# A two-layer graph network with attention: each load of q and k writes one of the two copies

## The chip, the cores and the metric

The kernel runs on one core of a Trainium2 chip. The metric is device time of one execution in microseconds (us). The core has a matrix engine (PE), a vector engine (DVE), an activation engine (ACT), a general engine (POOL, GpSimd) and a synchronisation engine (SP), which here only issues DMA transfers; the transfers themselves are carried out by 16 DMA engines that all queues share.

## The reference, cut to what matters

There are 3,327 nodes with 128 features and a dense adjacency matrix of zeros and ones. Layer 0 normalises the features, multiplies them by the transposed adjacency and by two small weights, normalises over the nodes and adds the result to x. Layer 1, in which nearly all the time goes, is an attention:

```python
q = (x @ Wq.T).reshape(d, n, h)          # d = 128 groups, n = 3327, h = 8
k = (x @ Wk.T).reshape(d, n, h)
v = (x @ Wv.T).reshape(d, n, h)
a = jnp.einsum('dnh,dmh->dnm', q, k) * scale
a = a + spatial_encoding + edge_encoding  # both are adj
a = jax.nn.softmax(a, axis=2)
out = jnp.einsum('dnm,dmh->dnh', a, v)
out = out.reshape(n, h * d)
return out @ Wo.T                         # added to x by the caller
```

So there are 128 independent attentions of 3,327 queries over 3,327 keys with a depth of only 8, and every score gets twice the adjacency entry added.

## The kernel before, in words

**Operands.** q and k are each split into a rounded part and a remainder (`projection`, lines 230 to 241), which are stored in DRAM as the 16 rows of `qT` and `kT`: rows 0 to 7 are the rounded part, rows 8 to 15 the remainder, one row for each h. A row holds all 128 groups, one after the other, and two rows are 425,984 numbers apart. In SBUF a group takes 32 partitions. Its q tile holds rounded, rounded, remainder, remainder; its k tile holds rounded, remainder, rounded, remainder. One product over 32 partitions thus sums all four part products. Every row of qT and kT is therefore needed twice in SBUF, and this repeat is what the change touches.

**Loops.** `attention` goes through 32 iterations i (`NG`), each for four groups (`G`), which lie in the four strips of 32 partitions. An iteration has seven blocks y of 480 queries (the last has 448) and in each 13 steps s, so 91 steps. A step treats two of the 26 chunks of 128 keys, for all four groups, as four (chunk, pair of groups) products in PSUM (`product`, line 785). Two or three of the four get the adjacency added by DVE from a tile `at` (line 925), and ACT takes the exponential of all of them at once (d, line 970). The others go through ACT first (f, line 934), and POOL multiplies them by weights `wt`, exponentials of the adjacency stored in DRAM as `wd` (line 937). PE then weighs v with the results, three steps later (`weigh`, line 670).

**Order.** The order of the instructions on each engine is written out by hand. SP issues its DMAs in program order, and a DMA that has to wait for a buffer or for data holds all behind it. `fetch` issues the loads of `at` (line 773, four buffers) and `wt` (line 769, three buffers) two steps ahead. `loads` (lines 167 to 202) makes the list of what the next iteration needs: for each half of the keys four loads of k into a staging tile `ks` (a pool with one buffer), then POOL copies (`sort`, line 194) that bring it into the order of the chunks in the k tile; v after the first half; and the q loads dealt out between the copies. All its DMAs have line 172. The list is spread evenly over the steps of the iteration, from step 4 on (step 39 in iteration 0):

```python
while pending and (total - len(pending)) * (SU * len(qblocks) - FROM[i] - 4) <= k * total:
    pending.pop(0)()
```

The q and k tiles have two sets, used in turn. In the same iteration the projections for the groups after the next are made piece by piece (`go_on`), and their stores to kT, qT and v1 (lines 247 and 222) stand in SP's order too. They wait for POOL, which splits the values.

**Start.** For iteration 0 `first_loads` (lines 873 to 901) loads the whole k of the four groups, straight into an unused tile, then the first 512 columns of q (line 883), then v; ACT, DVE and POOL sort k together (line 894). The rest of q (`others`, line 915) follows two loads a step from the third step on. In iteration 0 the weights wd of later blocks are also made: a load t (line 814), an exponential by ACT (line 819) and a store (line 806).

The helper `q_loads` gives two loads for a group (line 138 on): each writes 16 partitions from 8 rows with a leading repeat of 2. `k_loads` gives one load that writes 32 partitions from 16 rows with a leading repeat of 2.

Of the kernel before, what the change touches and what calls it, by code (L numbers as in the profile page):

```python
# [9 lines left out]
F32 = mybir.dt.float32  # L10
# [8 lines left out]
N = 3327  # L19
D = 128  # L20
H = 8
# [25 lines left out]
def tile_two_layer_gnn(  # L47
# [34 lines left out]
    kT = dram.tile([2 * H, TP], F32, name="kT")  # L82
# [55 lines left out]
    def q_loads(q, p0, d, n0=0, n=NP):  # L138

        qs = qT[:, bass.ds(d * N + n0, n)].rearrange("(a h) n -> a h n", h=H)  # L140
        return [
            (
                q[p0 + a * 2 * H : p0 + (a + 1) * 2 * H, n0 : n0 + n].bitcast(F32),
                qs[a].unsqueeze(0).to_broadcast([2, H, n]),
            )
            for a in range(2)
        ]

    def k_loads(k, p0, d, n0, n):
        ks = kT[:, bass.ds(d * N + n0, n)]  # L150
        return [(
            k[p0 : p0 + 4 * H].bitcast(F32), ks.unsqueeze(0).to_broadcast([2, 2 * H, n])
        )]

    def v_loads(v, d):
        W = NC * (H + 1)
# [10 lines left out]
    def loads(tiles, d):  # L167
# [6 lines left out]
        def batch(b):  # L174
            return d + b if b else d

        qs = [dma(*a) for b in range(G) for a in q_loads(q, 32 * b, batch(b))]
        vv = [dma(*a) for a in v_loads(v, d)]
        todo = []
        for half in range(2):  # L180

            ks = ksp.tile([P, NP // 2], F32R, name="ks")
            for b in range(G):
                todo += [
                    dma(*a)
                    for a in k_loads(ks, 32 * b, batch(b), half * (NP // 2), NP // 2)
                ]
            todo += vv if half == 0 else []
            todo += [qs.pop(0) for _ in range(2) if qs]
            for c in range(0, NC, 4):  # L190
                n = min(4, NC - c)

                def sort(ks=ks, c=c, n=n, half=half):
                    nc.gpsimd.tensor_copy(  # L194
                        k[:, c : c + n, half * 64 : half * 64 + 64],
                        ks.bitcast(F32).rearrange("g (p c) -> g c p", c=NC)[:, c : c + n, :],
                    )

                todo.append(sort)
                if qs:  # L200
                    todo.append(qs.pop(0))
# [107 lines left out]
    with tc.tile_pool(name="l0", bufs=1) as l0, tc.tile_pool(  # L309
# [16 lines left out]
        cols = l0.tile([P, 4], F32, name="cols")  # L326
# [162 lines left out]
        for c in range(NC):  # L489
            a = tiles[c]  # L490
# [37 lines left out]
            i = c - 2 * NQ - 5  # L528
# [4 lines left out]
        for n0 in range(0, NB, NB // 2):  # L533
            a = ap.tile([P, 7 * NB], F32, name="a")
# [174 lines left out]
    def attention():  # L709
# [3 lines left out]
        with tc.tile_pool(name="exd", bufs=4) as ep, tc.tile_pool(  # L713
# [13 lines left out]
            if True:  # L727
# [50 lines left out]
                def product(i, y, c, half):  # L778
# [13 lines left out]
                others = [  # L792
                    args for b in range(G)
                    for args in q_loads(sets[0][0], 32 * b, b, NB, NP - NB)
                ]
                late = None
# [76 lines left out]
                def first_loads():  # L873

                    q, k, v = sets[0]
                    ks = sets[1][1].rearrange("p c n -> p (c n)")
                    for b in range(G):
                        for args in k_loads(ks, 32 * b, b, 0, NP):
                            nc.sync.dma_start(*args)

                    for b in range(G):
                        for args in q_loads(q, 32 * b, b, 0, NB):
                            nc.sync.dma_start(*args)
                    for args in v_loads(v, 0):
                        nc.sync.dma_start(*args)

                    for c, copy in (
                        (16, nc.scalar.copy), (0, nc.vector.tensor_copy),
                        (4, nc.gpsimd.tensor_copy), (8, nc.scalar.copy),
                        (20, nc.vector.tensor_copy), (12, nc.gpsimd.tensor_copy),  # L890
                        (24, nc.vector.tensor_copy),
                    ):
                        n = min(4, NC - c)
                        copy(
                            k[:, c : c + n, :],
                            ks.bitcast(F32).rearrange("g (p c) -> g c p", c=NC)[:, c : c + n, :],
                        )
# [160 lines left out]
    def general():  # L1058
# [14 lines left out]
        with tc.tile_pool(name="sh", bufs=1) as sh, tc.tile_pool(  # L1073
# [4 lines left out]
            with tc.For_i(0, D, 1) as d:  # L1078
                q8 = sh.tile([4 * H, NP], F32R, name="q8")
                k8 = sh.tile([4 * H, NP], F32R, name="k8")  # L1080
                for args in q_loads(q8, 0, d) + k_loads(k8, 0, d, 0, NP):
                    nc.sync.dma_start(*args)
# [97 lines left out]
```

## Time and profile before

| | us |
|---|---|
| median of 3 runs | 10234.54 |
| lowest and highest run | 10231.9, 10239.35 |
| profiled execution | 10253.06 |
| its span, first to last instruction | 10251.3 |
| PE first multiplies q and k at | 263.24 |

The page counts 248 loads of ks and 248 loads of q on line 172, of 208 KB each; 4 of k (416 KB) and 8 of q (32 KB) at the start; and 8 of q (176 KB) on line 915. Together they are a small part of the 1,735.75 MB that the DMA moves. Most of that is 2,016 loads of at (480 KB, some 448) and 1,792 loads of wt (240 KB, some 224).

How to read it: busy time is the time an engine had an instruction in work. In a list of waits, "DVE d L925 <- DMA at" means that DVE stood idle before the instruction of line 925 until a transfer into at had landed. SP's own instructions only issue a transfer; their length is the time to issue, not to move.

### The profile page before, as it was taken

Reading aid. Unit: us, or ns where it says so; the run is one execution under the profiler, and the core shown is the slowest. Engines: PE = TensorE matmul, PEld = TensorE weight load, DVE = VectorE, ACT = ScalarE, POOL = GpSimd, SP = SyncE. Lnnn points to the kernel's source line nnn. Section 1 sums busy time; section 2 is a strip of 40 time slices with the busy share of each in tenths; the row PEclk is TensorE's granted clock in tenths of the full one; section 3 lists DMA queues with packets and bytes.
Section 4 is the critical chain, followed back from the end, with each engine's and each line's share of the span. In section 5 each row is a group of like instructions: output and inputs, shape, how many; then the busy total and the mean of one; then the engine's idle time right before and its main releaser. Section 6 shows DMA issues by size and latency. Waiting matters only on the chain.

```text
span 10251.3 us, 186610 instructions
## 1 busy us (share of the span) xinstructions
PE 9787.2 (95%) x71535; PEld 2720.9 (27%) x71535; DVE 9306.6 (91%) x9527; ACT 9886.6 (96%) x6662; POOL 8434.3 (82%) x4325
## 2 busy tenths in 40 slices
PE   7899999999999999999999999999999999999998
PEld 3122222222222222222222222222222222222222
DVE  5689999999999999999999999999999999999998
ACT  4799999999999999999999999999999999999998
POOL 1678888888888888888888888888888888888887
PEclk8899999999999999999999999999999999999999
DMA  6665666655666555666556665555666555656554
GB/s 238 195 188 162 169 173 169 170 164 164 169 173 170 168 165 165 170 171 168 168 161 167 168 174 168 164 168 163 170 169 170 167 163 168 171 167 170 162 158 129
DMA packets 1035806, 1735.75 MB, mean 169 GB/s; under 512 B 116086, under 2 KB 1011828, under 8 KB 1027092
## 3 DMA queue, kind: packets, MB, share of 16 engines
q1 hardware_dynamic: 1032399, 1718.85, 59.4%
q8 instruction: 561, 9.19, 0.4%
q0 software_dynamic: 784, 4.03, 0.1%
q14 instruction: 346, 2.83, 0.1%
q10 hardware_dynamic: 1716, 0.85, 0.0%
HBM read 1621.03 MB, written 102.37 MB: 168 GB/s over the span
## 4 chain that ended last, share of the span: by engine, by line
POOL 30%; PE 25%; ACT 20%; issue 11%; DMA 11%; DVE 2%; SPq 1%; POOLq 0%; ACTq 0%; DVEq 0%
POOL f L937 29%; PE av L670 13%; ACT f L934 11%; PE s L785 9%; ACT d L970 9%; DMA at<-in_adjT 6%; DMA wt<-wd 2%; DVE d L925 2%; PE acc L502 1%; DMA t<-in_adjT 1%; PE av L210 1%; POOL k L194 1%; DMA q<-qT 1%; POOL o L241 1%; POOL o L240 0%
## 5 line engine op out<-in xcount | busy, mean ns | idle before, releaser
L925 DVE SCALAR_TENSOR_TENSOR d<-at,s 128x960 f32<-128x960 f32 x8064 | 8733.3, 1138 | 632.9 <-PE s L785 361.2
L937 POOL TENSOR_TENSOR f<-f,wt 128x960 f32<-128x960 f32 (+1 forms) x3584 | 7933.3, 2233 | 1552.2 <-ACT f L934 1322.0
L970 ACT ACTIVATE d<-d 128x2880 f32<-128x2880 f32 (+1 forms) x2912 | 7071.3, 2428 | 97.0 <-DVE d L925 95.8
L670 PE MATMUL av<-d,v 128*9 128x480 f32 x32256 | 5126.0, 573 | 0.6 <-ACT d L970 0.6
L785 PE MATMUL s<-q,k 32*128 32x480 f32 x23296 | 4267.6, 479 | 412.8 <-ACT f L934 179.9
L934 ACT ACTIVATE f<-s 128x960 f32<-128x960 f32 (+1 forms) x3584 | 3443.7, 987 | 54.7 <-PE s L785 48.4
L785 PEld LDWEIGHTS s<-q,k 32*128 32x128 f32 x23296 | 1801.2, 183 | 5745.0 <-DVE d L925 3710.2
L670 PE MATMUL av<-f,v 128*9 128x480 f32 x14336 | 2876.7, 570 | 0.0
L670 PEld LDWEIGHTS av<-d,v 128*9 128x9 f32 x32256 | 585.1, 88 | 1228.0 <-issue 1226.1
L670 PEld LDWEIGHTS av<-f,v 128*9 128x9 f32 x14336 | 317.8, 88 | 154.0 <-issue 139.3
L194 POOL CAST k<-ks 128x256 fp32r<-128x256 f32 x434 | 284.2, 655 | 0.0
L241 POOL TENSOR_TENSOR o<-pf,o 104x512 fp32r<-104x512 f32 x124 | 159.5, 1287 | 9.9
L502 PE MATMUL acc<-a,A 128*128 128x512 f32 (+1 forms) x364 | 152.1, 570 | 9.2 <-DMA a<-in_adj 9.1
L680 DVE STREAM_TRANSPOSE avs<-av 128x480 f32<-128x480 f32 (+1 forms) x224 | 149.5, 667 | 4.4 <-PE av L670 4.4
L512 DVE TENSOR_REDUCE amax<-a 128x1 f32<-128x3327 f32 x26 | 93.7, 3604 | 27.8 <-DMA a<-in_adj 27.8
L444 POOL TENSOR_SCALAR o<-ident,rdeg 128x128 f32<-128x128 f32 x26 | 15.2, 601 | 110.1 <-DVE rdeg L441 110.1
L502 PEld LDWEIGHTS acc<-a,A 128*128 128x128 f32 x364 | 68.9, 192 | 94.9 <-issue 93.4
L509 ACT ACTIVATE junk<-a 128x3327 bf16<-128x3327 f32 x26 | 77.3, 2974 | 6.5 <-DMA a<-in_adj 6.5
L239 DVE TENSOR_SCALAR pf<-av,low_half 104x512 f32<-104x512 f32 x62 | 46.5, 751 | 40.0 <-PE av L210 38.8
L237 DVE COPY pf<-av 104x512 f32<-104x512 f32 x62 | 42.8, 691 | 39.5 <-PE av L210 39.5
L819 ACT ACTIVATE t<-t,low_half 128x960 f32<-128x960 f32 (+1 forms) x24 | 26.2, 1090 | 52.2 <-DMA t<-in_adjT 49.2
L240 POOL CAST o<-pf 104x512 fp32r<-104x512 f32 x124 | 76.1, 613 | 0.0
(131 smaller groups left out, 916.7 us busy)
## 6 DMA issues: line engine op xcount, KB each, us to landing
at<-in_adjT SPq DMA_DIRECT2D x1728, 480.0 KB
wt<-wd SPq DMA_DIRECT2D x1536, 240.0 KB
at<-in_adjT SPq DMA_DIRECT2D x288, 448.0 KB
wt<-wd SPq DMA_DIRECT2D x256, 224.0 KB
ks<-kT SPq DMA_DIRECT2D x248, 208.0 KB
q<-qT SPq DMA_DIRECT2D x248, 208.0 KB
a<-in_adj SPq DMA_DIRECT2D x26, 1663.5 KB
kT<-o SPq DMA_DIRECT2D x128, 208.0 KB
```

What stands on the lines that cost most here:

```text
L194: nc.gpsimd.tensor_copy(k[:, c : c + n, half * 64 : half * 64 + 64], ks.bitcast(F32).rearrange("g (p c) -> g c p", c=NC)[:, c : c + n, :],)
L210: nc.tensor.matmul(bank[:CH], hj, wqk[s][:, e * NB : (e + 1) * NB], start=True, stop=True)
L241: nc.gpsimd.tensor_tensor(o[:CH, 1], f[:CH], of[:CH, 0], ALU.subtract)
L502: nc.tensor.matmul(acc[i][:, :w], A[:, c, :], a[:, n0 : n0 + w], start=(c == 0), stop=(c == NC - 1),)
L512: nc.vector.tensor_reduce(amax[:, c : c + 1], a[:, :N], AX.X, ALU.max, apply_absolute_value=True)
L670: nc.tensor.matmul(av[32 * b : 32 * b + H + 1, :w], tiles[2][:, b, c, :], e, start=first, stop=last,)
L680: nc.vector.transpose(avs[:, :J, :].rearrange("p j h -> p (j h)"), av[:, : 32 * J].rearrange("p (q j) -> p j q", j=J),)
L785: nc.tensor.matmul(p[:, x, :we], k[rs, c, :], q[rs, n0 : n0 + we], start=True, stop=True,)
L925: nc.vector.scalar_tensor_tensor(d[:, j, :, :w], have[0, i, y, c // 2][:, c % 2, :w] .unsqueeze(1).to_broadcast([P, 2, w]), SAFE / 2, p[:, ...
L934: nc.scalar.activation(f[:, :, :w], p[:, :, :w], AF.Exp, scale=2.0)
L937: nc.gpsimd.tensor_tensor(f[:, :, :w], f[:, :, :w], have[1, i, y, c][:, :w].unsqueeze(1).to_broadcast([P, 2, w]), ALU.mult,)
L970: nc.scalar.activation(flat, flat, AF.Exp, scale=2.0)
```

## The change

Each load of q and k now writes one of the two copies. `q_loads` gives four loads for a group in place of two: 8 partitions each from 8 rows, load i from part i // 2. `k_loads` gives two in place of one: 16 partitions each from the 16 rows. No source has a repeated dimension any more. The same values reach the same places. All callers are unchanged: `loads`, `first_loads`, the list `others`, and two paths for scores that need a shift, which don't run with these inputs. The list of an iteration grows from 33 items to 49 (8 more of k, 8 more of q), spread over the same steps.

```diff
         qs = qT[:, bass.ds(d * N + n0, n)].rearrange("(a h) n -> a h n", h=H)
         return [
-            (
-                q[p0 + a * 2 * H : p0 + (a + 1) * 2 * H, n0 : n0 + n].bitcast(F32),
-                qs[a].unsqueeze(0).to_broadcast([2, H, n]),
-            )
-            for a in range(2)
+            (q[p0 + i * H : p0 + (i + 1) * H, n0 : n0 + n].bitcast(F32), qs[i // 2])
+            for i in range(4)
         ]
 
     def k_loads(k, p0, d, n0, n):
-        ks = kT[:, bass.ds(d * N + n0, n)]
-        return [(
-            k[p0 : p0 + 4 * H].bitcast(F32), ks.unsqueeze(0).to_broadcast([2, 2 * H, n])
-        )]
+        cols = bass.ds(d * N + n0, n)
+        return [
+            (k[p0 + i * 2 * H : p0 + (i + 1) * 2 * H].bitcast(F32), kT[:, cols])
+            for i in range(2)
+        ]
```

## The prediction

> **What bounds the kernel now.** I read the page first, then the totals of waits, then the timeline where the waits lie. Parts 1 and 4 of the page (busy time and share of each engine; the chain that ended last):
>
> ```profile
> span 10251.3 us, 186610 instructions
> PE 9787.2 (95%) x71535; PEld 2720.9 (27%) x71535; DVE 9306.6 (91%) x9527; ACT 9886.6 (96%) x6662; POOL 8434.3 (82%) x4325
> POOL 30%; PE 25%; ACT 20%; issue 11%; DMA 11%; DVE 2%; SPq 1%; POOLq 0%; ACTq 0%; DVEq 0%
> ```
>
> Four engines are nearly full and the chain wanders among them, so only a time in which all stand still can be won. DMA holds 11% of the chain, but that is transfer time, not loss. The loss is in the waits (total us, times, longest):
>
> ```profile
> POOL f L937 <- DMA wt<-wd: 200.6, 57, 10.6
> DVE d L925 <- DMA at<-in_adjT: 136.7, 98, 11.3
> ACT d L970 <- DVE d L925: 95.8, 99, 2.7
> ACT t L819 <- DMA t<-in_adjT: 49.2, 11, 19.7
> PE s L785 <- DMA q<-qT: 39.6, 2, 38.5
> ACT k L894 <- DMA k<-kT: 33.4, 1, 33.4
> ```
>
> To price them I took the ends of the 2,912 exponentials on d (L970), one a step. A quiet step takes 3.35 us (3.14 with 448 columns). Adding each step's fastest time over iterations 1 to 30 gives 303.2 us for an iteration of 91 steps. Those 30 iterations exceed that by 158.2 us in all (5.3 each): 3.45 an iteration in steps 11 to 18, 1.41 in steps 19 to 31, 0.4 elsewhere. The last iteration, which loads nothing ahead, has no such excess until its end. Iteration 0 takes 397.9, so 94.7 over; 24 exponentials of 1.09 us (L819), which add about 0.98 each to a step, explain 23.5 of it.
>
> What is late in steps 11 to 18 stands in the timeline of iteration 9 (start, us, engine, line; in brackets the idle time before):
>
> ```profile
> 3163.76 0.64 SPq L172 DMA_DIRECT2D ks<-kT  x1
> 3167.23 0.63 SPq L172 DMA_DIRECT2D ks<-kT  x1
> 3174.05 1.71 SPq L247 DMA_DIRECT2D kT<-o  x2
> 3175.85 1.20 SPq L773 DMA_DIRECT2D at<-in_adjT  x1
> 3184.32 3.28 DVE L925 SCALAR_TENSOR_TENSOR d<-at,s 128x960 f32<-128x960 f32 x3 [1.10 <-DMA at<-in_adjT]
> 3185.32 6.64 POOL L937 TENSOR_TENSOR f<-f,wt 128x960 f32<-128x960 f32 x3 [3.29 <-DMA wt<-wd]
> ```
>
> SP issues nothing from 3167.86 to 3174.05, held at a store that waits for POOL; then the at load needs 8.4 us to land. Why so long is seen at the start, where only the first k and q loads run (windows; the last two figures are the busy share of the 16 DMA engines and GB/s):
>
> ```profile
> 225.00:235.00 10.00, 0.00 (x0) 0.00 (x0) 1.13 (x3) 0.11 (x1) 1.05 (x2) 0.63 0.85 351
> 235.00:245.00 10.00, 0.00 (x0) 0.00 (x0) 0.00 (x0) 0.00 (x0) 0.00 (x0) 0.50 0.13 53
> 245.00:255.00 10.00, 0.00 (x0) 0.00 (x0) 0.00 (x0) 0.00 (x0) 0.00 (x0) 0.50 0.13 55
> ```
>
> 0.13 is 2 of 16 engines. A k or q load runs on two engines at 27 GB/s each, while the chip moves 351 GB/s when all take part.
>
> [...]
>
> **The change part by part.** Bytes stay the same, since the repeated source was read twice already. Each load becomes two.
>
> *SP's issues.* 248 q and 248 k loads in the loop, and 20 at the start, become twice as many: 516 more. A q or ks issue takes 0.64 now; a load of plain rows (wt) takes 0.34. At 0.34 the sum is 1032 x 0.34 - 516 x 0.64 = +21 us of SP, at 0.64 it is +330. I take the first. Either lies beside SP's own waits, 4306.6 us at L769 alone, so I cost it at nothing; if that cover were gone it would cost those 21 to 330.
>
> *Pacing.* loads() makes 49 items in place of 33, spread over the same 83 steps, so never two in a step after iteration 0. The last q load moves from step 55 to step 82 of 91: 9 steps, some 30 us, before its first use. The first sort of the second half stands three items after its last ks load instead of one, so POOL has more slack. The ks buffer is still free three steps before it is refilled. POOL makes the same 14 sorts (0.655 us each). Cost nothing, hidden under those margins.
>
> *A, the start.* The four k loads (1.70 MB) and eight q loads (0.26 MB) need 36 us on two engines (1.96 MB / 54 GB/s); k lands at 258.5, PE starts on s at 263.24. Spread, k needs some 5 to 7 us (1.70 MB at 351 or 259 GB/s, windows 225 and 205) from 215.3 and lands before 224. What is late next: ACT is busy to 225.1, DVE to 226.4, POOL to 226.8 with the layer before, then the same casts follow. They start 258.5 - 226.4 = 32 us earlier; PE, which waited for q 3.6 us more, could gain 36. But 3.4 MB of stores of hd and xd now share the DMA with the first steps. I take 32 (range 22 to 36).
>
> *B, iteration 0.* Its excess without the 23.5 is 71: about 22 in the first 11 steps, where the rest of q (eight loads of 176 KB, 26 us on two engines) holds an at load (11.3 and 5.5 us of DVE wait at 303 and 314); 11 in the steps without q or k loads, which stay; 38 from step 39 on, where k and q loads run beside wd's. I take 22 + 0.85 x 38 = 54 (range 25 to 71).
>
> *C, iterations 1 to 30.* A load of 208 KB will put 13 KB (k) or 26 KB (q) on an engine instead of 106 KB, 0.5 or 1 us instead of 4. The at load at 3175.85 then finds the stores and itself ahead, and by my estimate from the wait-free rates lands near 3180, before DVE wants it at 3183.2; wt likewise. That it is the backlog and not the hold on SP that costs shows in the same iteration: the first store of the pair (3160.58) also leaves 12 us without an at issue (3149.88 to 3162.32), with only one k load in the 20 us before it, and the four steps after it take 3.35 us each but for the 3.41 that every fourth or so takes anyway. I take 0.9 x 158 = 142 (range 0 to 158).
>
> Sum: 32 + 54 + 142 = 228. From the span of the profiled execution, 10251.3 - 228 = 10023; that execution took 10253.1 and the median of the runs is 10234.5, 18.6 less, and I carry the saving over unchanged: 10234.5 - 228 = **10006.5 us**.
>
> **Rivals.**
> *The hold on SP is the real cause.* Then C's excess stays, and only A, the 22 of B and some ten more go: 32 + 22 + 10 = 64, 10170 us. For it: at is issued 6 us late at each stall. Against it: the first store of each pair. Between the two, a gain with half of C: 10234.5 - 157 = 10078.
> *Everything goes.* 36 + 71 + 158 = 265: 9970 us. Against: the wd stores and 512-byte stores still share the queue.
> *The loads don't spread.* The program may still put them on two engines; the time stays near 10235 with 20 either way. [...]
> *SP becomes the bound (slower).* Place: SP between two at and wt issues. The trace has SP waiting for earlier, unrelated loads before it issues ("SPq L773 <- DMA ks<-kT", 75.1 us, 57 times), so more loads can mean more such holds. Price: 330 us if every extra issue costs 0.64 and all reach the path; with the 228 saved that ends at 10337. It decides from 228 / 516 = 0.44 us an extra issue on the path. Against: SP waits for buffers over half of the time, and the loads it waits for become shorter.
>
> **How the numbers follow.** Forecast (all but a little of C) 0.70, own range 9980 to 10050; half of C 0.08; SP's hold 0.09; everything and more 0.05; no spread 0.03; slower 0.05. The range 9970 to 10110 holds the forecast and half of C and leaves out the hold on SP, the upper ends of both signs and the gain beyond 265. Faster by over 0.2% (about what this kernel's measurement can tell from no change): 0.92; within 0.2%: 0.03; slower: 0.05.
>
> **What would show it.** Right: PE's wait for q at the start falls from 38.5 us to under 8 and the first s product starts near 230; the 0.13 stretch is gone; the waits of POOL for wt and of DVE for at fall below 60 and 40 us; steps 11 to 31 take 3.35 each; q and ks issues are 0.34 to 0.4 us. SP's waits for ks and q loads (75.1 and 58.4) nearly vanish. Wrong: at still lands 8 us after the second store of a pair (hold on SP or queue of stores), a step after a doubled issue is longer than 3.35, or a ks load still moves 54 GB/s.

## The result and the profile after

The kernel after takes 10068.93 us (median of 4 runs, 10065.25 to 10073.43) against 10236.94 us (10231.9 to 10239.62) for the kernel before beside it: a ratio of 0.9837, 95% interval 0.982 to 0.9854. The direction was forecast; the forecast of 10006.5 us was 62 us too low, though inside its range of 9970 to 10110.

The profiled execution took 10069.75 us. Its page, parts 1 and 4 (busy time and share of each engine; the chain that ended last):

```profile
span 10068.0 us, 187348 instructions
...
PE 9707.3 (96%) x71535; PEld 2723.1 (27%) x71535; DVE 9310.2 (92%) x9527; ACT 9879.0 (98%) x6662; POOL 8443.2 (84%) x4325
...
POOL 3%; ACT 2%; PE 2%; issue 1%; DMA 0%; DVE 0%; SPq 0%; POOLq 0%; ACTq 0%; DVEq 0%
```

The work is the same, so each engine has the same busy time and a higher share. Only PE's busy time fell, by 80 us with the same 71,535 products: some of them ran faster, which nothing in the prediction accounts for. The chain adds up to 8% of the span: it breaks off early, and nothing can be read from it. The totals of waits (us in total, times, longest) can be:

```profile
PE s L783 <- DMA q<-qT: 13.5, 2, 13.2
...
ACT t L817 <- DMA t<-in_adjT: 12.6, 7, 2.9
...
POOL f L935 <- DMA wt<-wd: 6.2, 11, 2.0
...
ACT k L892 <- DMA q<-qT: 4.0, 1, 4.0
...
DVE d L923 <- DMA at<-in_adjT: 2.9, 4, 1.4
```

POOL's wait for wt went from 200.6 us to 6.2, DVE's for at from 136.7 to 2.9, and the 33 us that ACT waited at the start before it could sort k to 4. PE still waits 13.2 us for q.

Iteration 9 has the same place in the order as the stretch shown of the kernel before. Its timeline of SP (start, us, engine, line):

```profile
3077.57 0.42 SPq L170 DMA_DIRECT2D ks<-kT  x1
...
3080.86 0.42 SPq L170 DMA_DIRECT2D ks<-kT  x1
...
3088.16 1.72 SPq L245 DMA_DIRECT2D kT<-o  x2
3089.98 0.41 SPq L771 DMA_DIRECT2D at<-in_adjT  x1
```

SP issues an at load at 3081.38, for 0.38, and then nothing until the store at 3088.16: held for 6.4 us, where it was 6.2 before. But the steps around it now end at 3087.8, 3091.2, 3094.5, 3097.9 and 3101.2, 3.3 to 3.4 us apart: nothing waits. Over the run, SP's waits for the values to store are not shorter than the 511.4 us of before; the totals of SP's own waits have

```profile
SPq L245 <- POOL o L238: 563.7, 124, 7.3
```

In three figures, from the ends of the exponentials on d as in the prediction ("excess" is the time above 303.2 us an iteration):

| us | before | after | gain | forecast |
|---|---|---|---|---|
| A: first exponential on d ends at | 272.1 | 246.1 | 26.0 | 32 |
| B: iteration 0 | 397.9 | 372.8 | 25.1 | 54 |
| C: excess of iterations 1 to 30 | 158.2 | 26.7 | 131.5 | 142 |
| what follows | | | 0.7 | 0 |

These sum to 183.3, the difference of the two spans. The medians of the runs differ by 168.0.

### The profile page after: what moved, and what is told of

Its sections match the earlier page's. It is cut to its first block, busy times and chain, and to the rows that moved or that the text cites. A ratio compares the mean times of both kernels' runs of the same rounds, so it can differ in the third digit from the quotient of the medians.

```text
span 10068.0 us, 187348 instructions
## 1 busy us (share of the span) xinstructions
PE 9707.3 (96%) x71535; PEld 2723.1 (27%) x71535; DVE 9310.2 (92%) x9527; ACT 9879.0 (98%) x6662; POOL 8443.2 (84%) x4325
## 3 DMA queue, kind: packets, MB, share of 16 engines
q1 hardware_dynamic: 1043655, 1718.90, 62.4%
## 5 line engine op out<-in xcount | busy, mean ns | idle before, releaser
L668 PE MATMUL av<-d,v 128*9 128x480 f32 x32256 | 5068.5, 567 | 0.6 <-ACT d L968 0.6
L442 POOL TENSOR_SCALAR o<-ident,rdeg 128x128 f32<-128x128 f32 x26 | 15.3, 604 | 111.7 <-DVE rdeg L439 111.7
L214 DVE COPY ov<-av 104x512 f32<-104x512 f32 x62 | 42.9, 692 | 36.0 <-PE av L208 36.0
```

What stands on the lines that cost most here:

```text
L668: nc.tensor.matmul(av[32 * b : 32 * b + H + 1, :w], tiles[2][:, b, c, :], e, start=first, stop=last,)
```

## The experiments

Two questions were open. Does the gain of C come from the spread over more engines (the forecast: a backlog on two engines), or from the other thing the change does, the new places of the loads in the order? And what is left at the start and in iteration 0? "Old places" are those of the kernel before, "new places" those of the kernel after. Each ratio is to the kernel before on the same chip; its median there was 10234 to 10259 us, so medians of different chips are less comparable than the ratios. The table collects the readings of the profiled executions; a "drop" is a stretch in iterations 1 to 30 in which the clock that the chip granted to PE is 0.50, half of full speed, with the total length of these stretches beside it.

| kernel | median us | ratio (95%) | first d ends | iteration 0 | excess 1-30 | of it steps 11-31 | drops, us |
|---|---|---|---|---|---|---|---|
| before | 10236.94 | 1 | 272.1 | 397.9 | 158.2 | 145.8 | 26, 187.7 |
| after | 10068.93 | 0.9837 (0.982-0.9854) | 246.1 | 372.8 | 26.7 | 6.6 | 2, 6.8 |
| e1_split2 | 10104.7 | 0.9857 (0.984-0.9873) | 272.7 | 382.9 | 25.1 | 8.8 | 2, 6.8 |
| e2_k_only | 10100.99 | 0.9851 (0.9834-0.9867) | 250.0 | 401.0 | 26.6 | 11.5 | 0 |
| e3_q_only | 10211.32 | 0.9964 (0.9952-0.9977) | 268.8 | 384.4 | 124.4 | 107.9 | 24, 105.8 |
| e4_inner | 10058.77 | 0.9811 (0.9794-0.9827) | 247.1 | 375.5 | 19.2 | 4.4 | 0 |
| e5_split2_paired | 10175.3 | 0.9942 (0.9925-0.9958) | 276.3 | 390.3 | 90.6 | 79.9 | 14, 71.7 |
| e6_after_paired | 10254.65 | 1.0018 (1.001-1.0027) | 243.7 | 369.8 | 211.9 | 4.3 | 56, 279.9 |
| e7_repaced | 10127.39 | 0.9896 (0.988-0.9913) | 272.5 | 404.0 | 31.4 | 9.0 | 2, 6.8 |
| e8_no_exp | 10007.73 | 0.978 (0.9761-0.98) | 243.1 | 322.4 | 17.1 | 4.3 | 0 |
| e9_paired_dup | 10135.17 | 0.9884 (0.9868-0.9901) | 248.2 | 367.5 | 87.2 | 3.6 | 1, 6.8 |
| e10_paired_shift | 10248.67 | 0.9993 (0.9984-1.0002) | 248.3 | 375.2 | 185.6 | 4.3 | 48, 211.6 |
| e11_pad | 10064.38 | 0.9813 (0.9793-0.9833) | 246.9 | 372.5 | 21.4 | 5.7 | 1, 3.4 |
| e12_best | 10063.62 | 0.9811 (0.9797-0.9824) | 251.3 | 367.6 | 21.9 | 5.0 | 0 |

### Twice the loads, still on two engines

e1_split2 gets its second load by cutting the columns in two. The repeat and the two engines stay; the list has 49 items, as after.

```diff
-    k[p0 : p0 + 4 * H].bitcast(F32), ks.unsqueeze(0).to_broadcast([2, 2 * H, n])
+    k[p0 : p0 + 4 * H, e * n // 2 : (e + 1) * n // 2].bitcast(F32),
+    ks[:, e * n // 2 : (e + 1) * n // 2].unsqueeze(0).to_broadcast([2, 2 * H, n // 2])
+    # for e in range(2); the q loads likewise
```

> As many loads as after (two for each of before), but cut along the columns, with the repeated source kept, so each should still run on two engines. Theory width (the number of engines that a load uses is what counts): nearly the time of before, within 25 us of 10237; two windows in the start at 0.13 of the DMA remain, and iterations 1 to 30 keep an excess of 130 to 170 us. Rival number and order (more, shorter loads and their new place among the copies free the queue): near 10069.

Measured: 0.9857, a gain of 146 us where the theory of width had almost none. The start is as before; a window between its loads of k and q (length, busy time and count of PE, PEld, DVE, ACT and POOL, granted PE clock, DMA share, GB/s) is

```profile
235.00:245.00 10.00, 0.00 (x0) 0.00 (x0) 0.00 (x0) 0.00 (x0) 0.00 (x0) 0.50 0.13 53
```

so the transfers still run on 2 of 16 engines. Yet the stalls of the loop are gone (totals of waits):

```profile
PE s L794 <- DMA q<-qT: 41.2, 2, 39.4
...
POOL f L946 <- DMA wt<-wd: 9.1, 8, 2.7
DVE d L934 <- DMA at<-in_adjT: 8.8, 3, 4.8
```

So the theory of width holds for the start and fails for the loop. The gain of C does not need the spread. It can come from smaller loads or from the new places.

### One operand at a time

e2_k_only changes `k_loads` alone and e3_q_only `q_loads` alone, each as in the diff of the change.

> k loads as after, q loads as before. Theory width: the stall after the k stores (steps 11 to 18, 103.6 us over 30 iterations) goes, the one after the q stores (steps 19 to 31, 42.2 us) stays at 35 to 60; the start gains most of its 26 us less the q wait of some 5; iteration 0 gains little, since the rest of q still runs on two engines in its first steps. Sum 110 to 135 us: 10102 to 10127. Rival: q and k gain alike, half of 168 each: 10153.

> q loads as after, k loads as before. Theory width: steps 11 to 18 keep 90 to 110 us of excess, steps 19 to 31 fall below 15; the start gains 0 to 8 us (k still needs 31 us on two engines); the first 11 steps of iteration 0 lose their stall of 20 us. Sum 45 to 70 us: 10167 to 10192. Rival: half of 168: 10153.

Measured: k alone gains 149 us (forecast 110 to 135), with all of C (excess 26.6) and most of the start (first d at 250.0); q alone gains 39 (forecast 45 to 70), and leaves an excess of 124.4. With k alone the second stall, in steps 19 to 31, went too (from 42.2 to 10.3), although the q loads there are those of before; but their places moved, since the list grew. With q alone, steps 11 to 18 keep 105.2 of 103.6, and steps 19 to 31 fall to 2.7. So each stall goes when the loads beside it become smaller or move, and these two runs don't say which.

### Halves at the old places

e5_split2_paired issues the two halves of e1_split2 back to back, as one item, where the kernel before has one load.

```diff
+        def two(args):
+            return [lambda x=x: [nc.sync.dma_start(*a) for a in x]
+                    for x in zip(args[::2], args[1::2])]
-                todo += [dma(*a) for a in k_loads(...)]
+                todo += two(k_loads(...))     # the q loads likewise
```

> The loads of the first experiment (cut along the columns, two engines), but the two halves of a load issued back to back in the place where before issues its one load (33 items in the list again). Theory lump (what the at loads queue behind is the bytes put on two engines between two held stores, whatever the number of loads): the stalls of iterations 1 to 30 come back, 110 to 180 us of excess, 10215 to 10245 in all. Rival number (shorter loads let others through): as the first experiment, near 10105.

Measured: 0.9942, 10175.3 us, between the two theories. The stalls are back, though shorter (totals of waits):

```profile
POOL f L949 <- DMA wt<-wd: 153.4, 56, 3.8
...
DVE d L937 <- DMA at<-in_adjT: 84.0, 79, 3.3
```

Against e1_split2 only the places differ: excess 90.6 against 25.1. Against before only the cut differs: 158.2. The longest waits fell from 10.6 and 11.3 us to 3.8 and 3.3. So the places matter, but the bytes alone don't set the stall: the same bytes in halves at the old places cost less, and why stays open.

### Whole loads at the new places

e7_repaced keeps the loads of before, whole and on two engines, and follows each in the list by an item that does nothing.

```diff
+        def none():
+            pass
-                    dma(*a)
+                    f
                     for a in k_loads(ks, 32 * b, batch(b), half * (NP // 2), NP // 2)
+                    for f in (dma(*a), none)     # the q loads likewise
```

> The loads of before, whole and on two engines, each followed by an empty item, so that they stand at the places of the first load of each pair of after (49 items). Theory lump: fewer whole loads fall between two held stores, so most of the excess of iterations 1 to 30 goes (20 to 70 us stay), the start stays: 10110 to 10165. Rival number: no gain, within 25 us of before. Rival width alone: no gain either.

Measured: 0.9896, 107 us by the medians, where the change gained 168. Excess 31.4, and in the totals of waits:

```profile
DVE d L932 <- DMA at<-in_adjT: 36.6, 24, 11.2
...
POOL f L944 <- DMA wt<-wd: 22.5, 7, 10.6
```

So new places suffice without any change to a load. The timeline of SP in iteration 9 of this kernel has

```profile
3136.51 0.82 SPq L254 DMA_DIRECT2D kT<-o  x2
...
3141.78 0.64 SPq L172 DMA_DIRECT2D ks<-kT  x1
...
3149.08 1.70 SPq L254 DMA_DIRECT2D kT<-o  x2
```

Only one ks load (3141.78) stands between the two kT stores that hold SP; before, two ks loads (3163.76, 3167.23) stood ahead of the held store at 3174.05. In the trace of before the rows of these two move one load after the other, mostly two rows at a time, from 3166.1 to 3172.7 us and from 3175.7 to 3180.6. By this reading, which no run tests alone, the stall needs two such loads just ahead of a hold of SP.

### Spread loads at the old places

e6_after_paired is the mirror image: the loads of the kernel after, issued in pairs at the old places with the same `two`.

> The loads of after, but the two copies issued back to back in the places of before (33 items). Theory lump: spread over 8 or 16 engines there is no lump in any place, the excess of iterations 1 to 30 stays under 45 us, 10055 to 10090. Rival pacing (the new places in the list are the whole gain of the loop): the excess comes back to over 100 us, 10150 or more.

Measured: 1.0018 (12 runs, 10232.02 to 10261.33). That is the time the rival forecast, but not for its reason. As the backlog theory has it, the transfers are no longer late (totals of waits):

```profile
POOL f L938 <- DMA wt<-wd: 12.6, 7, 4.7
```

and DVE's waits for at don't appear at all. But 199.7 us of excess stand in steps 32 to 60, where before had under 5. Windows of one such place (columns as above):

```profile
1990.90:1994.30 3.40, 1.92 (x14) 0.53 (x14) 2.35 (x3) 3.40 (x5) 3.23 (x2) 1.00 0.78 210
1994.30:2001.10 6.80, 6.64 (x34) 1.25 (x34) 4.26 (x4) 3.54 (x4) 3.38 (x2) 0.50 0.48 105
2001.10:2004.50 3.40, 3.40 (x28) 0.80 (x24) 2.79 (x4) 3.40 (x4) 2.25 (x1) 1.00 0.27 93
```

PE pauses for 1.5 of 3.4 us; in the next 6.8 us it is full and does 34 products, where the 3.4 us after that hold 28. Its granted clock was 0.50 meanwhile. The clock drops 56 times in the 30 iterations, 26 times at step 42 and 29 at step 52.

The kernel before has the same thing at its stall. Windows of its iteration 2, step 14:

```profile
1026.00:1029.80 3.80, 3.13 (x24) 0.76 (x24) 1.76 (x3) 3.27 (x2) 0.27 (x1) 1.00 1.08 295
1029.80:1033.20 3.40, 1.97 (x16) 0.65 (x16) 3.40 (x4) 2.24 (x1) 2.63 (x2) 1.00 1.01 297
1033.20:1040.00 6.80, 6.80 (x34) 1.22 (x34) 4.68 (x5) 6.13 (x6) 6.80 (x4) 0.50 0.44 137
1040.00:1043.40 3.40, 3.40 (x28) 0.80 (x24) 2.78 (x4) 2.25 (x3) 1.68 (x2) 1.00 0.43 88
```

First the late transfers (DMA share 1.08 and 1.01), with PE idle for 1.4 us; then, with the DMA share down to 0.44, 6.8 us at half clock. The stall is paid twice. The 26 stretches at half clock in iterations 1 to 30 of before last 3.41, 6.83 or 10.24 us (7, 9 and 10 of them), and from 700 us on every change of the granted clock in before, after and e6_after_paired lies within 0.5% of a window on a grid of 3.413 us. Ahead of the drops in the two places shown, PE was busy for 1.92 (e6_after_paired) and 1.97 (before) of 3.40 us, a share of 0.56 and 0.58. In e6_after_paired 56 of the 57 grid windows with a share under 0.62 were followed by a drop, in before 23 of 26. The exact condition stays open: in before, windows at 0.49 and 0.52 were not followed by a drop, and drops followed windows at 0.65 and 0.86.

### Keeping PE busy in the pause

If the half clock costs the 200 us of e6_after_paired, or most of them, then more work for PE must make that kernel faster. e9_paired_dup adds, to e6_after_paired, some s products computed twice in steps 42, 43, 52 and 53.

```diff
-                    for x in range(2):
+                    for x in (0, 1, 0, 1) if twice else (0, 1):
...
+                    busy = (y, s) in ((3, 3), (3, 4), (4, 0), (4, 1))
-                    add(0, product(i, y, *plain[0]))
+                    add(0, product(i, y, *plain[0], busy))
```

> The pairs of the sixth run, with the s products of steps 42, 43, 52 and 53 of each iteration partly computed twice into the same place (the result is the same), so that PE has more to do where its clock fell. Theory clock (a stretch of 3.4 us in which PE is busy under some 0.6 halves its clock, and that is the whole 199.7 us of the new excess): drops at 42 and 52 fall from 55 to under 15, the excess of iterations 1 to 30 to under 90, 10050 to 10130 in all. Rival POOL (the k sort of these two steps is what holds the path, the clock only follows): 10220 or more, since PE gets more work and POOL none less.

Measured: 0.9884, faster than without the added work by 119 us by the medians (the two ran on different chips) and by 137 by the ratios; one drop is left. A window around one of the places where e6_after_paired has its pause:

```profile
1984.00:2004.00 20.00, 19.86 (x156) 5.35 (x148) 19.55 (x22) 19.17 (x13) 16.40 (x9) 1.00 0.62 145
```

That shows the mechanism: with PE kept busy the clock stays up, and most of the loss is gone. It is not the whole 199.7 us, as the theory had it: 77.0 us of excess stay in steps 32 to 60 without half clock, from the pause itself or from the added products, which the runs don't separate.

The price of a us at half clock is an estimate. 124.7 us less excess (211.9 - 87.2) for 273 us less at half clock (279.9 - 6.8) is 0.46 each. Within e6_after_paired, the two iterations with 3.4 us at half clock take 308.1 us and the 26 with 10.2 take 310.6: 2.5 / 6.8 = 0.37. The 187.7 us of the kernel before are then worth 69 to 86. Its own iterations give 90: the 22 with a drop take 309.6 us on average, the 8 without 305.5, 22 x 4.1 = 90. That is too much if anything, since the iterations with a drop also wait longer for at and wt (11.3 us of DVE and POOL together, against 6.3). So half to two thirds of the 131.5 us that C gained was time at half clock, and the rest, by this account, the late transfers themselves.

e10_paired_shift asks what makes the pause in e6_after_paired, by moving its whole list one step later past the sorts on POOL.

```diff
-    FROM = [3 * SU] + [LAG + 1] * (NG - 1)
+    FROM = [3 * SU] + [LAG + 2] * (NG - 1)
```

> The pairs of the sixth run, with the list started one step later in iterations 1 to 30, so that the sorts leave steps 42 and 52. Theory coincidence (sort and that step together open the pause): the drops at 42 and 52 go, excess under 60, 10045 to 10095. Rival lock (an iteration without DMA stalls settles on a length of 91 windows of 3.413 us wherever the sorts stand): drops at other steps, 10150 or more.

Measured: 0.9993, with 48 drops, 45 of them at the same steps 42 and 52. The sorts moved by one to two steps and the pause did not, so their coincidence with these steps is not it. Nor is a transfer waited for there. What opens the pause stays open.

### What the repeat itself costs

e4_inner has as many k loads as the kernel after and as many q loads as the kernel before. It keeps a repeat, but inside: both copies of a row of q come from one load, whose rows lead; k is read by row and part.

```diff
-                qs[a].unsqueeze(0).to_broadcast([2, H, n]),
+                qs[a].unsqueeze(1).to_broadcast([H, 2, n]),
...
+        ks = kT[:, bass.ds(d * N + n0, n)].rearrange("(a h) n -> h a n", h=H)
+        # two loads of 16 partitions from ks in place of one of 32
```

> Two q loads a group, as before, with the repeated source kept, but the repeat stands inside and the 8 rows lead; two k loads a group whose 16 rows are read as 8 by 2. The rows lie in another order in q and k alike, so the sums of products hold the same terms. [...] Theory width: within 20 us of after (10069), with 256 fewer issues of q. Rival that the repeat itself is what slows a load: the q stalls of steps 19 to 31 and of the first steps come back, 10110 or more.

Measured: 0.9811 (0.9794 to 0.9827), the fastest complete kernel at 10058.77 us; its interval overlaps that of the change. No stretch at 0.13 is left at the start: from 235 to 245 us, where the kernel before has 0.13, the DMA share is 0.83. A repeat that does not lead costs nothing that shows in the total. Its issues take 0.70 us each, against 0.33 for q and 0.42 for ks in the kernel after, and lie beside SP's waits.

### The start and iteration 0

After the change k lands near 229 and PE starts at 238.23. The timeline of the start (as above; in brackets the idle time before):

```profile
215.29 4.56 SPq L877 DMA_DIRECT2D k<-kT  x8
219.90 15.97 SPq L881 DMA_DIRECT2D q<-qT  x16
...
238.23 0.73 PE L783 MATMUL s<-q,k 32*128 32x480 f32 x1 [13.22 <-DMA q<-qT]
```

Windows of it, columns as above:

```profile
220.00:225.00 5.00, 4.47 (x22) 3.57 (x22) 2.89 (x10) 4.89 (x12) 3.87 (x8) 0.60 1.01 160
...
230.00:235.00 5.00, 0.00 (x0) 0.00 (x0) 2.96 (x3) 1.72 (x2) 2.70 (x2) 0.50 1.02 428
```

All 16 engines are busy in both (1.01, 1.02), but from 220 to 225 they move only 160 GB/s, and from 230 to 235 428 GB/s of something else than q, for which PE waits. The DMA queues from 228 to 236 us (packets, MB, share of 16 engines) say of what:

```profile
q0 software_dynamic: 392, 3.11, 92.8%
q1 hardware_dynamic: 131, 0.13, 6.0%
```

The stores of hd and xd, on POOL's queue, have 93% of the engines; the 16 q loads, on SP's, move 0.13 MB in 8 us. SP adds to it: it takes from 219.90 to 235.87 to issue these 16 loads, since it waits before an issue for an earlier k or q load to land (7.4 us in 7 waits for k, 2.2 in 3 for q), so the last one leaves only 2.4 us before PE starts. How much of PE's 13.2 us is the stores' share and how much SP's hold was not separated.

e11_pad asks whether the slow k reads come from the distance between the rows of kT, which a pad of 4 KB changes.

```diff
-    kT = dram.tile([2 * H, TP], F32, name="kT")
+    kT = dram.tile([2 * H, TP + 1024], F32, name="kT")     # qT likewise
```

> After, with 4 KB between the rows of qT and kT, so that rows are no longer 13 times 128 KB apart. Theory rows (16 engines that read 16 rows at this distance hold each other up: 1254 ns for a row of 13,312 bytes at the start against 498 on two engines): the median falls under 800 ns and k lands 3 to 5 us earlier; the total moves by under 10 us, 10055 to 10072. Rival ([...]the stores of the layer before, whatever the distance): 1100 ns or more.

Measured: no. A row of 13 KB takes 1361 ns (median) there, 1248 over all rows in the kernel after, where up to 16 of them move at once, 866 in e4_inner, and 498 in the kernel before, where mostly two do. The distance between the rows is not the cause; what is stays open.

e8_no_exp leaves out the exponentials of the weights wd of the later blocks (their loads and stores stay), so it doesn't compute these weights.

```diff
-                        nc.scalar.activation(a, a, AF.Exp, bias=low, scale=2.0)
+                        pass
```

> After without the 24 exponentials of line 817 in iteration 0: the weights wd of blocks 1 to 6 are then stored without their exponential, all else runs. Theory clock: iteration 0's excess of 69.6 us is these 23.5 us and what the slower PE clock costs after the pauses that they make; without them it falls to 10 to 30 and few clock drops remain: 10010 to 10035. Rival DMA (transfers of t and wd still hold the others): an excess of 40 or more stays, 10045.

Measured: 0.978. Iteration 0 falls by 50.4 us to 322.4. The exponentials' own time explains 23.5 of it; the time at half clock in iteration 0 falls from 58.0 us to 6.8, which at 0.37 to 0.46 is 19 to 24 more. Most of what iteration 0 still loses is not transfers.

e12_best puts two things on e4_inner: the first q loads go ahead of those of k, and some s products are computed twice in the steps of iteration 0 that have such an exponential.

```diff
+                        for args in q_loads(q, 32 * b, b, 0, NB):     # ahead of k_loads
...
+                    busy = i == 0 and s % 3 == 2
```

> The loads of the fourth run (the repeat inside, two q and two k loads a group, eight engines), with the first q loads ahead of the first k loads, and in iteration 0 two of the four s products computed twice in the steps that carry an exponential of the weights, into the same place. Theory start (the first q, issued last and 16 KB a load, stands behind the stores of hd and xd): PE's wait for q falls from 13.2 us to under 4 and the first exponential on d ends 6 to 10 us earlier, near 238. Theory clock: iteration 0 falls from 375.5 to 345 to 360, with fewer than 5 clock drops instead of 11. In all 10025 to 10045. Rival: the stores hold k in q's stead and the start stays at 245 to 248; PE in iteration 0 waits for ACT in any case and the doubled products gain nothing: 10055 to 10065.

Measured: 10063.62 us, 0.9811 (0.9797 to 0.9824): no better than e4_inner. Iteration 0 gained 7.9 us, the start lost 4.2, since now k is late instead of q:

```profile
ACT k L895 <- DMA k<-kT: 17.3, 1, 17.3
```

The order of the loads moves the wait from one to the other. In iteration 0 nine drops stay, where under five were expected.

## Why the prediction was right or wrong

**"Pacing. ... Cost nothing, hidden under those margins": wrong, and the largest miss of the mechanism.** The paragraph asked whether the new places do harm, not whether they do good. e7_repaced has only the new places, gains 107 us and takes 126.8 of C's 131.5; e1_split2 has them with loads on two engines and leaves as little excess as the change. What the spread adds to that is the start and some of iteration 0: against e1_split2, 26.6 us and 10.1 us.

**C, 142 forecast, 131.5 measured: the size is right, the mechanism half right.** The "backlog and not the hold on SP" is confirmed as far as the at loads go: SP is held as long as before (563.7 us), and nothing waits. The hold alone is not the cause. But the backlog is only late where two loads stand just ahead of a hold, so either cure takes it away, the spread (e6_after_paired) or the places (e7_repaced). And half to two thirds of C, by the estimates above, was not waiting at all, but PE at half clock after the wait. The prediction counted this as wait because it summed the lengths of steps; the record of the granted clock, which it had, would have shown it. The size held since the two go together when the wait goes; that no new pause of PE came in its place was luck, as e6_after_paired shows: the spread alone, with the stalls gone, and no gain. The number of engines behind "13 KB (k) or 26 KB (q) on an engine" was the author's estimate; the trace of the kernel after has up to 16 rows of ks and up to 8 of q on the move at once in the loop, where the kernel before has mostly two.

**A, 32 forecast, 26.0 measured.** The 0.13 stretch went, as said. "k needs some 5 to 7 us ... and lands before 224" failed: rows that took 498 ns, mostly two at once, take 1248 with up to sixteen at once, and k lands near 229. The text named the 3.4 MB of stores of hd and xd as a cost, and it is q that they hold, with SP's late issues: PE's wait fell to 13.2, not "under 8", and the first product starts at 238, not 230.

**B, 54 forecast, 25.1 measured.** By steps of iteration 0 the excess went from 26.1 to 11.8 (first 11 steps, forecast gain 22, measured 14.3), from 19.9 to 16.7, and from 48.7 to 41.1 (from step 39 on, forecast gain 32, measured 7.6). "38 from step 39 on, where k and q loads run beside wd's" put on transfers what e8_no_exp shows to be mostly the exponentials: without them the excess from step 39 on falls from 41.1 to 12.4. Of the 50.4 us that go in all, what lies beyond their own 23.5 is about what the half clock costs.

**"I carry the saving over unchanged": 15 us.** The profiled execution of the kernel before was 16 us above its runs, that of the kernel after less than 1. The time of the kernel before also depends more on the run: 15 runs on one chip lie between 10221.72 and 10247.94 us, and the mean granted clock goes with it, 0.984 in the fastest and 0.981 in the slowest. So the runs differ in their time at half clock, of which the kernel after has hardly any left in iterations 1 to 30 (6.8 us). That the profiled execution was one with more of it fits (0.981); the clocks of the runs beside it are not on record.

The misses add up: 6.0 in A, 28.9 in B, 10.5 in C, less 0.7, 15.3 in the carrying over and 2.4 in the median of before make the 62.4 us.

**Right:** the issues (0.33 us for q and 0.42 for ks, from 0.64) cost nothing visible; no extra issue makes SP the bound; SP's waits for q and ks loads are gone in the loop; the waits for wt (6.2) and at (2.9) are far under 60 and 40, and the steps at the old stall take 3.35 to 3.41.

## What to carry to other kernels

A change that multiplies transfers also moves them in the order; that half deserves a forecast of its own, and one run with the old transfers at the new places separates the two. When a trace shows a stall, look at the granted clock in the few microseconds after it: at 95% load, pauses like the one of 1.4 us cost, by the estimates above, at least as much afterwards as while they lasted. And a change that makes transfers faster can open a pause elsewhere; it is won only when no new pause of PE comes with it.

## What the runs showed that was not expected

- One 3.413-us window with PE busy under 0.62 of the time was nearly always followed by 3.4 to 10.2 us at half clock (56 of 57 such windows in e6_after_paired, 23 of 26 in before). In e6_after_paired 26 of the 30 iterations take 310.6 to 310.8 us, about 91 such windows (310.6), so that the grid can meet the pause at the same point in one iteration after the other; this is argued, not shown.
- Computing some products twice made a kernel faster by some 120 us (e9_paired_dup against e6_after_paired).
- Stores with rows of 5 to 13 KB on POOL's queue took 93% of the DMA engines, small q loads on SP's 6%, for at least 8 us.
- A 13-KB row of k at the start takes 498 ns in before, where mostly two such rows move at once, 866 in e4_inner and 1248 in after, where up to 16 do. The loads together still become faster: k lands near 229 instead of at 258.5.
